# A transformer block on one core: four tiles for the split projections, the first maxima's rows and an exponential inside the projections, score products in attention's first two steps, and the first biases in the last unit

## The chip, the core and the metric

The kernel runs on one core of a Trainium2 chip. The metric is the device time of one launch in microseconds (us). TensorE is called PE here and its weight loads PEld; VectorE is DVE, ScalarE is ACT, GpSimd is POOL, and SP is the engine that issues most of the DMA transfers.

## What is computed

The reference is one block of a diffusion transformer with a conditioned layer norm, causal attention and an MLP, all in fp32. Here there are B = 2 rows of T = 2048 tokens with D = 512 channels, 16 heads of 32, and 2048 hidden channels.

```python
mod = silu(condition) @ Wada + bada
sh_a, sc_a, gt_a, sh_m, sc_m, gt_m = split(mod, 6, axis=1)
xm = layernorm(x, g1, be1) * (1.0 + sc_a[:, None, :]) + sh_a[:, None, :]
q, k, v = heads(xm @ Wqkv)
scores = where(causal, q @ k.T * hd ** -0.5, -inf)
attn = softmax(scores) @ v
x = x + gt_a[:, None, :] * (attn @ Wproj + bproj)
xm = layernorm(x, g2, be2) * (1.0 + sc_m[:, None, :]) + sh_m[:, None, :]
h = gelu(xm @ W1 + b1)
x = x + gt_m[:, None, :] * (h @ W2 + b2)
```

## The kernel before

**Stages.** For each of the two rows: the projections to q, k and v, then attention, then the out-projection; the MLP follows for both rows together. The out-projection of row 0 is `project_phase`, whose hook `between` prepares the projections of row 1.

**Projections** (`Qkv`). They run in four groups g of 512 tokens. `group` has twelve parts n: n = 0 to 7 are q and k for four sets of four heads in turn (`ps_qk`), n = 8 to 11 are the values (`ps_v`) of four token tiles. Each q or k is split in two: ACT writes the high part into `hl` (L808[...]), DVE the rest (L809), and SP stores both to DRAM (L814), from where q and k come back as `qst` and `kst` with the parts laid over the partitions. `hl` has two tiles. `load_x` fetches the tokens of the group after into four tiles `x` (L759), and `stats` (L212) takes their mean and variance on DVE. Row 1's projections also carry a preparation of the MLP's weights on POOL.

**Units and scores.** Attention works in 16 units per row, four heads by 512 queries: unit u is a head set c and a query block i, with the blocks in order 0, 1, 2, 3 for the first set and 0, 2, 1, 3 for the others. A unit has two kinds of products. The *score products* (`Row.score`, tiles `s`) are done ahead of time only to find each query's largest score: DVE reduces them with L452, or with L447 where the causal mask is added. They have two PSUM banks of their own, `ps_s`, and can borrow one of the others. When the last of a unit is reduced, `split` (L466 to L468) writes the maxima in two parts to `mhl`. `rows(u)` then transposes them on PE (`ps_m`), and DVE spreads them into `fold` (L512). Score products of the first three units are interleaved with the products of the projections' groups 1 to 3 (the hook `among`, and `count`, which says how many are due).

**Steps.** A unit with query block i has 4i + 3 *steps*, 144 per row in all. A step first puts the negative maxima into four banks with four *bias products* (st<-fold,sel), adds the products of keys and queries (st<-kst,qst, keys on the partitions), and lets ACT write the four exponentials `e` (L577). On the diagonal, POOL zeroes what the mask hides (L583, affine_select). The products with the values (`o`) follow LAG = 2 steps later, and those with ones (`sm`), which sum the exponentials, come after them; pairs or more of exponentials are first added into `ee` (L605), on POOL, in the last unit on DVE. `due` spreads the score products of later units, at most AHEAD = 3 units ahead, over the steps, by a table of costs written in the kernel. The limit is one unit shorter in a unit's first two steps:

```python
n = row.count(
    due(u, starts[u] + n_step) - QB // 2, u + AHEAD - (n_step < 2)
)
```

**The last unit and the out-projection.** In the last unit of a row, `prepare` runs once per step and loads and scales what the out-projection needs: the weight, the gate, the bias `bgate`, the first query block's output `at_s[0]` (times its inverse sums, L427), and the first four token tiles `xt_s`. These four lie in the old `kst` tile, and so appear as kst in the profile. The out-projection takes 16 token tiles n, four to each query block (k counts the blocks). For each one POOL adds the bias to the tokens (L972), PE multiplies (`ps_o`), DVE adds the two (L979), and one part of the next block's output is scaled (L985).

**Order.** Each engine runs its instructions in one order. That of the matmuls, and of what is wrapped in `act`, is the order written; a scheduler orders the rest, DMA issues on SP among them. Code lines at the spot of the change are shown below.

Of the kernel before, what the change touches and what calls it, by code (L numbers as in the profile page):

```python
# [8 lines left out]
F32 = mybir.dt.float32  # L9
F32R = mybir.dt.float32r  # L10
BF16 = mybir.dt.bfloat16
AF = mybir.ActivationFunctionType
ALU = mybir.AluOpType
# [4 lines left out]
P = 128  # L18
# [3 lines left out]
QB = 512  # L22
MT = 512
# [4 lines left out]
def dit_block_kernel(  # L28
# [36 lines left out]
    nc = tc.nc  # L65
# [5 lines left out]
    HC = P // HD  # L71
# [4 lines left out]
    LAG = 2  # L76
# [54 lines left out]
        nc.vector.tensor_copy(pick, pickc.unsqueeze(3).to_broadcast([P, 2, B, P]))  # L131


    first_sqrt = const.tile([P, 1], F32, tag="first", name="first")
    nc.scalar.activation(first_sqrt, eps, AF.Sqrt)


    cols = const.tile([P, 64], F32, tag="cols", name="cols")
# [63 lines left out]
    def act(ins):  # L202

        return tc.keep_in_program_order(ins)
# [78 lines left out]
    class Row:  # L283
# [125 lines left out]
        def prepare(self, n):  # L409

            if n == 3:
                self.prefetch()
            elif n == 5:
                ps = rows_of(ps_sp, 0, self.b, "s")
                self.rb_s = [self.old_queries() for _ in range(2)]
                self.gate = self.rb_s[1][:, 0, :]
                act(nc.vector.tensor_copy(self.gate, ps))
                act(nc.vector.tensor_tensor(bgate, bgate, self.gate, ALU.mult))
                nc.sync.dma_start(self.rb_s[0], wide_d[self.b][last_order[0]])
            if 6 <= n < 6 + C:  # L420
                w = self.wproj[:, n - 6, :]
                act(nc.vector.tensor_tensor(w, w, self.gate, ALU.mult))
            if n == 10:
                nc.sync.dma_start(self.rb_s[1], wide_d[self.b][last_order[1]])
            if 11 <= n < 11 + C:
                d, r = self.at_s[0][:, n - 11, :], self.rb_s[0][:, n - 11, :]
                act(nc.vector.tensor_tensor(d, d, r, ALU.mult))  # L427

# [98 lines left out]
    def attention_phase(row):  # L527
        b, vv, kst, qst = row.b, row.vv, row.kst, row.qst
        with pool(f"att{b}") as ap, pool(
# [136 lines left out]
            for u, (c, i) in enumerate(units):  # L666
                if NQ <= u + AHEAD < len(units):
                    row.load_queries(u + AHEAD)
                if u % NQ == 0 and c + 1 < C:
                    row.load_keys(c + 1, 0, NG)  # L670
                steps = len(steps_of[u])
                for n_step, tiles in enumerate(steps_of[u]):
                    last = n_step == steps - 1
                    if n_step == 0:
                        summed = set()
                        o = ps_op.tile([P, QB], F32, tag="o", name="o")
                        sm = ps_op.tile([P, QB], F32, tag="sm", name="sm")
                    ready = row.at

                    n = row.count(  # L680
                        due(u, starts[u] + n_step) - QB // 2, u + AHEAD - (n_step < 2)
                    )
                    es, rest = scores_t(u, n_step, n)
                    rest = len(row.todo) - rest
                    make_rows = False
                    if u + 1 < len(units) and row.rows_made == u + 1:
                        if last:
                            row.score(row.count(cum[-1], u + 1))
                        make_rows = last or (ready > u + 1 and n_step >= 1)
                    row.inverses(u, n_step)  # L690
                    if u == len(units) - 1:
                        row.prepare(n_step)
                    flush(now)
                    if make_rows:
                        row.rows(u + 1)
                    row.score(max(0, len(row.todo) - rest))

                    def tile_by_tile(dst, lhs, es, tiles, first, last):
                        at = 0
                        for n, (j, q) in enumerate(tiles):  # L700
                            products(
                                dst, lambda h: lhs(j, h), es, q, at,
                                first and n == 0, last and n == len(tiles) - 1,
                            )
                            at += QB - q

                    def values(es=es, tiles=tiles, c=c, o=o, first=n_step == 0, last=last):
                        tile_by_tile(
                            o,
                            lambda j, h: vv[:, j, (c * HC + h) * HD : (c * HC + h + 1) * HD],  # L710
                            es, tiles, first, last,
                        )

                    def row_sums(es, last, tiles=((0, 0),), sm=sm, summed=summed):
                        first = not summed
                        summed.add(len(summed))
                        tile_by_tile(sm, lambda j, h: ones[:, :HD], es, tiles, first, last)

                    pending.append((now + LAG, values))
                    sums_of, wait = None, 0  # L720
                    if n_step < i * TQ:
                        k = n_step % TQ
                        if k == 0:
                            even = es
                        elif k == 1:
                            chain = begin_chain(u, even, es)
                        else:
                            add_to(u, chain, es)
                        if k == TQ - 1 and n_step + 1 < i * TQ:
                            sums_of, wait = (chain, False), 2  # L730
                    elif i and n_step == i * TQ:
                        add_to(u, chain, es)
                        sums_of, wait = (chain, False), 2
                    else:

                        sums_of, wait = (es, last, tiles), i > 0 and not last
                    if sums_of:
                        pending.append(
                            (now + LAG + wait, lambda f=row_sums, s=sums_of: f(*s))
                        )  # L740
                    if last:
                        pending.append((now + LAG, lambda u=u, o=o, sm=sm: finish(u, o, sm)))
                    pending.sort(key=lambda p: p[0])
                    now += 1
            flush(now + LAG)

    class Qkv:
# [41 lines left out]
        def group(self, g, hp, between, among):  # L789
# [6 lines left out]
            for f in range(C):  # L796
                for which in range(2):
                    ps = psum.tile([P, MT], F32, tag="mm", name="ps_qk")
                    w0 = which * D + f * P
                    for k in range(C):  # L800
                        mm(
                            ps, w[:, k, w0 : w0 + P], xmT[:, k, :],
                            start=(k == 0), stop=(k == C - 1),
                        )
                        among(n, k)
                    hl = hp.tile([P, 2, MT], F32R, tag="hl", name="hl", bufs=2)
                    scale = HD**-0.5 if which == 0 else 1.0
                    nc.scalar.activation(hl[:, 0, :], ps, AF.Copy, scale=scale)  # L808
                    nc.vector.scalar_tensor_tensor(  # L809
                        hl[:, 1, :], ps, scale, hl[:, 0, :].bitcast(F32),  # L810
                        ALU.mult, ALU.subtract,
                    )
                    dst = (qd if which == 0 else kd)[b][f]
                    nc.sync.dma_start(  # L814
                        dst[:, :, tok].rearrange("l p t -> p l t"), hl.bitcast(F32)
                    )
                    between(n)
                    n += 1
                if f == 0:
                    row.load_keys(0, g)  # L820
                    row.load_queries(g)
# [12 lines left out]
        def run(self, hp, also):  # L834

            row = self.row
            for g in range(NG):

                def between(n):
                    if g + 1 < NG:  # L840
                        if n == 0 and g + 1 not in self.xts:
                            self.load_x(g + 1)
                        if n in (5, 8):
                            self.norm(g + 1, n // 8)()
                    also(g, n)

                def among(n, k):
# [13 lines left out]
                            )  # L861

                self.group(g, hp, between, among)
            row.rows(0)

    w1_v = W1.rearrange("(c p) f -> p c f", p=P)
    w2_v = W2.rearrange("(c p) f -> p c f", p=P)
# [62 lines left out]
    def project_phase(row, psum, between):  # L930
# [5 lines left out]
        with pool(f"proj{b}") as pp:  # L936
# [14 lines left out]
            for k, i in enumerate(last_order):  # L951
# [6 lines left out]
                for t in range(TQ):  # L958
# [10 lines left out]

                    tokens(n + 6)  # L970
                    nt, xt = rows_x[n], xts[n]
                    act(nc.gpsimd.tensor_tensor(xt, xt, bgate, ALU.add))  # L972
                    ps = psum.tile([P, D], F32, tag="mm", name="ps_o")
                    for c in range(C):
                        mm(
# [139 lines left out]
    attention_phase(row)  # L1115


    first, row = row, Row(1)
    with pool("qkv1") as qp, pool("ps_qkv1", bufs=6, space=PSUM) as ps_mm:
        qkv = Qkv(row, qp, ps_mm)  # L1120
        qkv.xts[0] = first.next_s

        def between(n):
            if n == 6:
# [8 lines left out]
            if n >= NT - MTT:  # L1133
                qkv.stats(1, n - (NT - MTT), True)

        project_phase(first, ps_mm, between)

        def also(g, n):
            if n % 4 == 1:
# [361 lines left out]
```

## Time and profile before

| | |
|---|---|
| runs | 2432.94, 2437.04, 2436.72 us, median 2436.72 |
| profiled execution | 2439.56 us, of which the span is 2437.9 |
| PE busy | 2394.4 us (98%), 10797 instructions |
| DVE, POOL, ACT busy | 1349.5 (55%), 1091.5 (45%), 893.7 (37%) |
| row 0: projections, attention, out-projection | 18.7 to 219.0, to 764.5, to 823.7 us |
| row 1: projections, attention, out-projection | 823.7 to 1021, to 1567, to 1626.5 us |
| MLP | 1626.5 to 2437 us |
| four exponentials / one POOL add / one select | 2.07 / 1.27 / 0.3 to 0.5 us |

In a timeline, a row gives the start and the length in us, the engine, the line, the operation with what it writes and reads, how many instructions are taken together, and in brackets how long the engine had been idle before and what released it. In a table of windows, a row gives for each engine the busy time and the number of instructions in that window, then PE's granted clock (1.00 is full speed), the mean busy share of the DMA engines, and GB/s. PE's matmul records are stretched while it waits for a bank or an operand, so a busy PE can still be one that waits.

### The profile page before, as it was taken

To read this page: it belongs to the slowest core of one execution; us is meant where nothing else is said; L and a number is where in the kernel's file an instruction comes from. 1 tells how busy PE (TensorE), PEld (TensorE's weight loads), DVE (VectorE), ACT (ScalarE), POOL (GpSimd) and SP (SyncE) were. 2 spreads that over 40 slices of the span, in tenths; PEclk is the share of its full clock that TensorE was granted. 3 is DMA by queue.
4 is the path that set the end of the run, shared out by engine and by line. 5 is a ranking of instruction groups with operands and counts; after the bars stand their busy time and mean duration, and the time that the engine had idled before them with its cause. 6 is when DMAs were issued, how large, how long until landed. Compare 5 with 4: busy or idle time off the path is not lost.

```text
span 2437.9 us, 31025 instructions
## 1 busy us (share of the span) xinstructions
PE 2394.4 (98%) x10797; PEld 1172.4 (48%) x10797; DVE 1349.5 (55%) x2836; ACT 893.7 (37%) x1668; POOL 1091.5 (45%) x1255
## 2 busy tenths in 40 slices
PE   8999999999999999999999999999999999999998
PEld 3445555555544444555555554444444444444443
DVE  3465766767657535567666665673354263343424
ACT  2212555555554021255555555423213212312310
POOL 1061997978773460089787879312002101100200
PEclk9999999999999999999999999999999999999999
DMA  7667115051325694530515122462234234222323
GB/s 227 218 224 194 41 39 114 23 113 45 104 95 207 211 303 158 149 67 23 123 35 113 45 78 105 145 204 76 87 99 132 88 96 141 82 91 94 115 85 99
DMA packets 132853, 285.72 MB, mean 117 GB/s; under 512 B 13472, under 2 KB 42700, under 8 KB 127832
## 3 DMA queue, kind: packets, MB, share of 16 engines
q1 hardware_dynamic: 126224, 257.46, 35.6%
q0 software_dynamic: 6384, 26.25, 3.0%
q8 instruction: 85, 1.39, 0.2%
q14 instruction: 72, 0.59, 0.1%
q10 hardware_dynamic: 88, 0.02, 0.0%
HBM read 209.76 MB, written 81.79 MB: 120 GB/s over the span
## 4 chain that ended last, share of the span: by engine, by line
PE 94%; DVE 2%; DMA 2%; POOL 1%; issue 1%; ACT 0%; DVEq 0%; SPq 0%; ACTq 0%; POOLq 0%
PE st L200 20%; PE ps_y L200 16%; PE ps_h L200 16%; PE o L200 11%; PE s L200 10%; PE ps_qk L200 9%; PE ps_o L200 4%; PE sm L200 4%; PE ps_v L200 4%; DMA k<-hl 1%; PE ps_xt L208 1%; POOL ee L605 1%; PE ps_o L208 0%; DVE junk L447 0%; DMA x<-in_x_dram 0%
## 5 line engine op out<-in xcount | busy, mean ns | idle before, releaser
L577 ACT ACTIVATE e<-st 128x512 f32<-128x512 f32 (+1 forms) x1152 | 573.8, 579 | 432.5 <-PE st L200 364.4
L605 POOL TENSOR_TENSOR ee<-ee,e 128x512 f32<-128x512 f32 x424 | 528.8, 1285 | 4.8 <-ACT e L577 4.5
L452 DVE TENSOR_REDUCE mx<-s 128x1 f32<-128x512 f32 x606 | 408.9, 688 | 206.3 <-PE s L200 205.3
L200 PE MATMUL s<-kst,qst 128*128 128x512 f32 (+3 forms) x1032 | 464.9, 452 | 9.0 <-DVE mx L447 4.2
L200 PE MATMUL st<-qst,kst 128*128 128x512 f32 (+3 forms) x1280 | 412.5, 390 | 0.0
L1272 POOL TENSOR_TENSOR c<-c 128x512 f32<-128x512 f32 x32 | 40.8, 1274 | 623.7 <-DVE c L1234 487.6
L200 PE MATMUL o<-e,vv 128*32 128x512 f32 (+3 forms) x2560 | 296.9, 540 | 2.0 <-POOL e L583 2.0
L447 DVE CUSTOM_DVE_ANT_0 junk<-s,causal 128x512 bf16<-128x512 f32 (+3 forms) x426 | 209.2, 491 | 147.1 <-PE s L200 139.1
L200 PE MATMUL ps_h<-sx,w 128*128 128x512 f32 x640 | 286.7, 592 | 0.0
L200 PE MATMUL ps_y<-sh,w 128*128 128x512 f32 x640 | 278.3, 595 | 0.0
L200 PEld LDWEIGHTS st<-qst,kst 128*128 128x128 f32 x1280 | 230.0, 190 | 94.9 <-issue 62.9
L200 PEld LDWEIGHTS s<-kst,qst 128*128 128x128 f32 x1032 | 194.9, 189 | 158.3 <-DVE mx L452 49.5
L605 POOL TENSOR_TENSOR ee<-e 128x512 f32<-128x512 f32 x168 | 210.3, 1284 | 105.6 <-ACT e L577 105.3
L200 PE MATMUL ps_qk<-xmT,wqkv 128*128 128x512 f32 x512 | 242.3, 601 | 2.2 <-DVE xmT L257 2.2
L583 POOL TENSOR_SCALAR_AFFINE_SELECT e<-e 128x128 f32<-128x128 f32 (+1 forms) x384 | 119.7, 347 | 255.8 <-ACT e L577 253.0
L1234 DVE TENSOR_TENSOR h<-c,ps_h 128x512 f32<-128x512 f32 x128 | 88.0, 688 | 232.4 <-PE ps_h L200 232.2
L200 PEld LDWEIGHTS ps_h<-sx,w 128*128 128x128 f32 x640 | 121.1, 190 | 150.2 <-issue 149.5
L200 PEld LDWEIGHTS ps_y<-sh,w 128*128 128x128 f32 x640 | 121.3, 191 | 148.9 <-issue 147.5
L1258 ACT ACTIVATE h<-h,cols 128x512 f32<-128x512 f32 x128 | 92.4, 722 | 182.0 <-DVE h L1234 182.0
L200 PE MATMUL st<-fold,sel 32*128 32x512 f32 (+1 forms) x1152 | 150.7, 483 | 2.1 <-DVE mhl L468 1.0
L200 PEld LDWEIGHTS ps_qk<-xmT,wqkv 128*128 128x128 f32 x512 | 95.0, 192 | 99.0 <-issue 92.6
L200 PEld LDWEIGHTS st<-fold,sel 32*128 32x128 f32 x1152 | 60.1, 182 | 148.1 <-ACT e L577 91.2
(128 smaller groups left out, 2325.8 us busy)
## 6 DMA issues: line engine op xcount, KB each, us to landing
qst<-q SPq DMA_DIRECT2D x128, 256.0 KB
w<-w1d SPq DMA_DIRECT2D x34, 896.0 KB
w<-w2d SPq DMA_DIRECT2D x28, 1024.0 KB
kst<-k SPq DMA_DIRECT2D x24, 1024.0 KB
q<-hl SPq DMA_DIRECT2D x32, 512.0 KB
k<-hl SPq DMA_DIRECT2D x32, 512.0 KB
kst<-k SPq DMA_DIRECT2D x32, 256.0 KB
w<-in_L_cond_W_dram POOLq DMA_DIRECT2D x64, 128.0 KB, 4.7
```

The costliest lines, as they stand in the source:

```text
L200: return tc.keep_in_program_order(nc.tensor.matmul(*args, **kw))
L208: return tc.keep_in_program_order(nc.tensor.transpose(dst, src, ident[:n, :n]))
L447: nc.vector.tensor_tensor_reduce(junk[:, :w], s[:, :w], causal[:, QB - w :], 1.0, MASKED, ALU.add, ALU.max, m,)
L452: nc.vector.tensor_reduce(m, s[:, :w], axis=AX.X, op=ALU.max)
L577: act(nc.scalar.activation(e[:, :w], sts[h][:, :w], AF.Exp))
L583: nc.gpsimd.affine_select(d, d, pattern=[[0, len(tiles)], [1, P]], compare_op=ALU.is_ge, fill=0.0, base=0, channel_multiplier=-1,)
L605: act(engine.tensor_tensor(dst, x, y, ALU.add))
L1234: nc.vector.tensor_tensor(dst, x, y, op)
L1258: nc.scalar.activation(d, d, AF.Gelu, bias=col(r_b1 + chunk, 1))
L1272: nc.gpsimd.tensor_tensor(c1_, c1_, c2_, ALU.subtract)
```

## The change

There are four edits, and a renaming (`first_sqrt` to `first`, and the row `first` to `past`). The tiles `hl` are four instead of two. The rows of the first unit's maxima are made in the last group of the projections, after its first value product, instead of behind the group, and ACT there takes one exponential of a column that nobody reads, so that its function table is loaded at that point. In the first two steps of a row's attention at least four score products may be placed, and unit 3, the third ahead, is open to them. POOL's four additions of the bias to the first block's tokens are issued in the last four steps of the last unit, in `prepare`, instead of in the out-projection.

```diff
--- before.py
+++ after.py
@@ -131,8 +131,8 @@
         nc.vector.tensor_copy(pick, pickc.unsqueeze(3).to_broadcast([P, 2, B, P]))
 
 
-    first_sqrt = const.tile([P, 1], F32, tag="first", name="first")
-    nc.scalar.activation(first_sqrt, eps, AF.Sqrt)
+    first = const.tile([P, 1], F32, tag="first", name="first")
+    nc.scalar.activation(first, eps, AF.Sqrt)
 
 
     cols = const.tile([P, 64], F32, tag="cols", name="cols")
@@ -423,6 +423,9 @@
             if n == 10:
                 nc.sync.dma_start(self.rb_s[1], wide_d[self.b][last_order[1]])
             if 11 <= n < 11 + C:
+
+                t = self.xt_s[n - 11]
+                act(nc.gpsimd.tensor_tensor(t, t, bgate, ALU.add))
                 d, r = self.at_s[0][:, n - 11, :], self.rb_s[0][:, n - 11, :]
                 act(nc.vector.tensor_tensor(d, d, r, ALU.mult))
 
@@ -678,8 +681,12 @@
                     ready = row.at
 
                     n = row.count(
-                        due(u, starts[u] + n_step) - QB // 2, u + AHEAD - (n_step < 2)
+                        due(u, starts[u] + n_step) - QB // 2,
+                        u + AHEAD - (n_step < 2 and u > 0),
                     )
+                    if u == 0 and n_step < LAG:
+
+                        n = max(n, HC)
                     es, rest = scores_t(u, n_step, n)
                     rest = len(row.todo) - rest
                     make_rows = False
@@ -803,7 +810,7 @@
                             start=(k == 0), stop=(k == C - 1),
                         )
                         among(n, k)
-                    hl = hp.tile([P, 2, MT], F32R, tag="hl", name="hl", bufs=2)
+                    hl = hp.tile([P, 2, MT], F32R, tag="hl", name="hl", bufs=4)
                     scale = HD**-0.5 if which == 0 else 1.0
                     nc.scalar.activation(hl[:, 0, :], ps, AF.Copy, scale=scale)
                     nc.vector.scalar_tensor_tensor(
@@ -842,6 +849,10 @@
                             self.load_x(g + 1)
                         if n in (5, 8):
                             self.norm(g + 1, n // 8)()
+                    elif n == 8:
+
+                        row.rows(0)
+                        act(nc.scalar.activation(first, eps, AF.Exp))
                     also(g, n)
 
                 def among(n, k):
@@ -861,7 +872,6 @@
                             )
 
                 self.group(g, hp, between, among)
-            row.rows(0)
 
     w1_v = W1.rearrange("(c p) f -> p c f", p=P)
     w2_v = W2.rearrange("(c p) f -> p c f", p=P)
@@ -969,7 +979,8 @@
 
                     tokens(n + 6)
                     nt, xt = rows_x[n], xts[n]
-                    act(nc.gpsimd.tensor_tensor(xt, xt, bgate, ALU.add))
+                    if k > 0:
+                        act(nc.gpsimd.tensor_tensor(xt, xt, bgate, ALU.add))
                     ps = psum.tile([P, D], F32, tag="mm", name="ps_o")
                     for c in range(C):
                         mm(
@@ -1115,10 +1126,10 @@
     attention_phase(row)
 
 
-    first, row = row, Row(1)
+    past, row = row, Row(1)
     with pool("qkv1") as qp, pool("ps_qkv1", bufs=6, space=PSUM) as ps_mm:
         qkv = Qkv(row, qp, ps_mm)
-        qkv.xts[0] = first.next_s
+        qkv.xts[0] = past.next_s
 
         def between(n):
             if n == 6:
@@ -1133,7 +1144,7 @@
             if n >= NT - MTT:
                 qkv.stats(1, n - (NT - MTT), True)
 
-        project_phase(first, ps_mm, between)
+        project_phase(past, ps_mm, between)
 
         def also(g, n):
             if n % 4 == 1:
```

## The prediction

> **What bounds the kernel now.** I read the chain of waits first, then busy time and granted clock in windows cut at the stages, then the timelines of the places where PE stops or slows, and the chain behind each.
>
> ```profile
> PE 94%; DVE 2%; DMA 2%; POOL 1%; issue 1%; ACT 0%; DVEq 0%; SPq 0%; ACTq 0%; POOLq 0%
> ...
> 18.70:219.00 200.30, 195.87 (x566) 95.66 (x566) 98.68 (x238) 36.11 (x66) 41.24 (x60) 0.99 0.66 210
> 219.00:240.00 21.00, 19.99 (x104) 10.83 (x103) 7.63 (x18) 9.62 (x18) 3.95 (x12) 0.76 0.89 188
> 240.00:764.50 524.50, 521.34 (x3568) 269.38 (x3566) 356.29 (x849) 295.40 (x591) 425.90 (x479) 1.00 0.28 74
> ...
> 223.88:227.29 3.41, 3.41 (x10) 2.47 (x10) 0.00 (x0) 1.81 (x5) 1.11 (x4) 0.50 1.02 207
> 227.29:230.71 3.42, 3.42 (x13) 2.53 (x13) 1.51 (x3) 1.90 (x5) 1.54 (x5) 0.50 0.96 196
> 230.71:234.12 3.41, 3.41 (x19) 0.85 (x18) 1.33 (x3) 0.66 (x2) 0.83 (x3) 0.50 1.05 226
> ...
> 882.59:886.00 3.41, 3.41 (x6) 1.33 (x4) 0.85 (x3) 0.00 (x0) 1.83 (x4) 0.51 0.98 363
> ```
>
> After the times come the engines PE, PEld, DVE, ACT, POOL, then clock, DMA share and GB/s. PE owns the chain, so only PE's stops and slow stretches can be won. The attention body runs at clock 1.00, but its first 21 us hold 0.76: three windows at half clock (row 1 the same, 1025.94 to 1036.17, 0.50). One more lies in row 1's projections.
>
> ```profile
> 161.11 0.60 ACT L808 ACTIVATE hl<-ps_qk 128x512 fp32r<-128x512 f32 x1 [2.74 <-DMA k<-hl]
> 163.27 0.50 PE L200 MATMUL s<-kst,qst 128*128 128x512 f32 x1 [2.32 <-DVE mx L452]
> 221.57 0.51 PE L200 MATMUL st<-fold,sel 32*128 32x512 f32 x4 [1.01 <-DVE mhl L468]
> 879.85 0.69 DVE L212 BATCH_NORM_STATS2 stat<-x 128x6 f32<-128x512 f32 x1 [3.26 <-DMA x<-in_x_dram]
> 881.61 0.44 PE L200 MATMUL s<-kst,qst 128*128 128x384 f32 x1 [3.39 <-DVE mx L447]
> ```
>
> PE's stops name a DVE reduction. What held DVE is ahead of it in its own queue: the low half of hl (L809), which waits for ACT's high half (L808), which waits until an earlier hl has been stored.
>
> **1. hl in four tiles.** Nothing is added to any engine; ACT's and DVE's turns for a tile come two tiles later. Row 0: chain DMA k<-hl 155.14 + 5.89, ACT, DVE, PE at 163.27; the 2.32 goes whole: a tile takes eight products of 0.43 (ps_qk 4.29 per ten in the chain), 3.4 us, so four span 13.7. Row 1: hl's stores took 15.09 (from 846.00) and 8.71 us (863.29), which held SP back, so that the x load left only at 873.87 and DVE's L212 waited for it until 879.85. The 3.39 goes, and with it half of the half-clock window 882.59:886.00, 1.7 us. The edit reorders SP: in row 1 three x loads stand behind the next group's first q store instead of around the last k stores, and on DVE their L212 come behind two reductions of that group. At 875.5 (first q done) plus the landing of 5.89 they are there by 882. DVE then frees the third score bank, which PE wants for its fifth product; by row 0's spacing (71.84, 72.81, 74.64, 77.40, 83.12) that is 11.3 us after 874.85, at 886. The 15.09 can still outlast 13.7; ACT's 1.4 is then covered by the projections' six banks. So nothing new should stop PE; I allow 1.0 for a partial wait over both rows. If the cover of 4 us fails, each us of lateness beyond it is one of PE. Sum -7.4 + 1.0 = -6.4; bounds -7.5 and, with a new wait as long as the old one in row 1 (3.39 + 1.7) and none gone in row 0, about 0.
>
> **2. First maxima's rows and an Exp inside the projections.** Before, the transpose ps_m comes after the last value product (220.29), the fold (L512, DVE 0.83) follows, and PE stands 1.01 (row 1: 0.92 at 1022.95). Afterwards both lie among the last group's products, where a transpose of 0.27 goes between score products and 0.83 on a DVE half idle (98.68 of 200.30) costs nothing. PE can then start the bias products at once, but the third waits for a bank that the last value copy (ACT 220.49 to 221.07) frees, so 0.55 of each gap is won: -1.1 over both rows. The table load (1.28 at 221.09) ends at 222.37, before the first product is there: the first exp starts 0.17 behind it. Moving it gains nothing by this row; ACT is 18% busy where it goes.
>
> **3. Score products in the first two steps.** The instruction order before and after gives, per row, score products in steps 0 and 1: 0 and 0 before, 5 and 5 after; in steps 36 and 37 (the next head group's first two): 5 and 4 before, 0 and 0 after; in between the counts move by one, from step 38 on they are equal. Both places are PE's. At 36 and 37, nine products of 0.225 (a 512-wide one there) are 2.0 us; steps start at 359.74, 363.56, 369.20, and ACT's four exps (2.07) fit in what is left, so PE can run 2.0 earlier. Against it: POOL works from 324.59 to 363.98 without a pause over 0.6 and its twelve selects (3.49 from 360.49) release the next value products; I take 1.8 per row. At steps 0 and 1 the added 2.2 us fall into PE's waits for exps (ACT 2.07 per four, PE's own work 1.7), so they cost little: step 0 to step 3 lasts 13.0 us in the trace (221.57 to 234.58), of which 7.4 would be work at full clock.
>
> The clock decides the rest. The window 220.47 to 223.88 ahead of those at half clock holds the 1.01 gap and waits for banks; by counting instructions at their unhindered times PE truly worked some 47% of it. Elsewhere a gap of 2.32 (163.27) and one of 1.73 (782.83) were followed by no drop; that last one left about 51% idle at worst. So what tips the clock here is near half a window. With edits 2 and 3 I count 65 to 70% of work in these windows. The page "TensorE: Matmul & The Clock Gate" of the Trainium skill, section "Part 1: The HAM clock gate", speaks against it: half clock follows a whole idle window of about 3.4 us, and its end table asks for no gaps over about 3 us. By that rule neither the 1.01 gap nor this filling matters, the drop has some other cause and stays, and edit 3 is worth about -2.0 per row with edit 2. By the trace (3.39 agrees with the rule, 1.01 contradicts it) the drop goes: I lay the steps out at full clock with the ten products and reach step 3 2.7 us earlier than 234.58 (the 0.55 of edit 2 in it). I take the trace: -2.7 - 1.8 = -4.5 per row, -9.0 over both for edits 2 and 3. Bounds -3.4 (clock still halves, part of steps 36 and 37 given back) and -11.
>
> **4. First biases earlier.** Four POOL adds per row move from the out-projection (L972, 4.97 from 761.87) into the last unit's last four steps. Where they were, they hid: DVE's first use (L979, 768.33) waits for PE, and POOL stands until 770.71 afterwards. So leaving costs and wins nothing. Where they go, each (1.24) stands in POOL's queue between the selects of one step and the next: the first in 34.83 us of idle before 755.40, harmless; the second behind 757.5, delaying the eight selects of 758.08 by about 0.7; the third delays the last four by up to 1.5. The value products that wait for them start 760.02 and 763.49, behind other products. For DVE's two-input adds in the same stretch (L605 0.69, L427 0.69), the nearest rows are L985 next to L972: 0.66 alone, 1.66 and 2.49 beside POOL's. The page "SBUF — State Buffer", section "SBUF: two separate sides", names it an exclusive lock between POOL and two-input DVE operations, for the whole instruction: by it each bias can cost DVE 1.24, five us of DVE time per row; by the rows 1.0 to 1.8 for one that meets. L427's last is due only for the products at 764.52 and was done by 760.27, so 4 us cover it. I put +0.3 per row, bounds 0 and +1.5; a gain is excluded since the adds were hidden.
>
> The renaming costs nothing. **Sum:** -6.4 - 9.0 + 0.6 = -14.8 against the profiled execution's 2439.56 (span 2437.9 and 1.66 around it): 2424.8. That execution lies 2.84 above the median of the runs, 2436.72, so on their scale 2421.9; I say 2422.5. Runs spread over 4 us, so a difference of 0.2% (4.9 us) is about what a measurement can tell from no change.
>
> **The rivals.**
> - Main case, 0.56: both halves hold, 2418 to 2427, middle 2422.5.
> - The clock still halves at the start, or POOL gives steps 36 and 37 back, 0.24: edits 2 and 3 bring -4 instead of -9, and 2436.7 - 6.4 - 4 + 0.6 = 2427. For it: the page's rule, and POOL's 39 us without a pause. Against: occupancy over the level of 782.83, where no drop came.
> - DVE waits for the later x loads, 0.13: edit 1 brings 0 to -3 and the clock part is partly lost too: 2436.7 - 1.5 - 4 + 0.6 = 2431.8. For it: DMA share 0.97 to 1.06 around 880, stores of up to 15 us. Against: 4 us of cover.
> - Slower, 0.07: one mechanism, the x loads that now follow a group's first q store, three places in all (two in row 0, one in row 1). If they land after the 15.09 that a store took there, instead of 5.89, they come at 890.6, DVE frees the bank at 891.6 instead of by 886, PE stands 5.6 and half of a window at half clock (1.7) follows: 7.3 a place. Two places give 2421.5 (the sum without its allowance) + 14.6 = 2436, no change; all three 2443. So it decides from a landing near 14.5 us at all three. Against: the loads around 157 to 164 landed with 5.89 at 301 GB/s.
> - That the change does not do what it says is small: the order of instructions shows the ten products, the four tiles and the earlier rows.
>
> **How the numbers follow.** Faster by over 0.2% is below 2431.8: the main case, the second, and half of the third less tails, 0.80. Within 0.2%: the rest of the third and the near side of the fourth, 0.13. Slower: 0.07. The range takes in the main case with edit 3's deep bound, the second, and the middle of the third: 2417 to 2432.5.
>
> **What would show it.** Right: no PE gap over 1 us at about 163 and 880; ACT no longer waiting for DMA q or k<-hl; first bias products directly behind the last value products, granted clock near 1.0 there; steps 0 to 3 in about 10 us; steps 36 and 37 shorter by 2. Wrong: clock 0.50 at the start of attention again, DVE L212 waiting for DMA x by over 3 us with PE behind it, POOL's selects named as releaser at the value products of steps 35 to 37, or out-projection products waiting for L427.

## The result, and the profile after

The changed kernel takes 2424.3 us (median of 4 runs, 2422.69 to 2425.71), the kernel before beside it 2436.88 (2432.94 to 2438.42): a ratio of 0.9951, with a 95% interval of 0.9933 to 0.9968. The prediction was 2422.5, range 2417 to 2432.5. The profiled executions went from 2439.56 to 2424.88, -14.7, where the sum said -14.8. That these two agree is in part luck. By the stretches of the table below, the projections won 9.3 us (1.07 and 8.26) where the `hl` term said 6.4, attention up to its last step 9.2 where 9.0 was said, and the ends of the last units lost 3.8 where 0.6 was said: two errors of opposite sign. And the profiled execution before lies 2.7 us above its kernel's median; from median to median the change won 12.6 us, where the prediction had 14.2 (2436.72 to 2422.5).

Windows of the changed kernel: 21 us at each start of attention (first two rows; row 0's is the window shown before), and a stretch of row 0's projections:

```profile
219.00:240.00 21.00, 19.94 (x139) 11.48 (x139) 14.50 (x34) 11.39 (x23) 7.10 (x15) 1.00 0.96 199
1010.00:1031.00 21.00, 20.18 (x141) 11.40 (x140) 15.23 (x34) 11.65 (x24) 7.38 (x15) 1.00 0.91 192
...
133.11:136.52 3.41, 3.41 (x8) 1.65 (x7) 1.12 (x4) 0.00 (x0) 2.16 (x4) 0.60 1.06 327
```

PE's clock at the start of attention is 1.00 in both rows (0.76 before in row 0), with 139 PE instructions in row 0's 21 us instead of 104. A stretch at reduced clock now lies at 133 us, where the profile before had none.

The timeline of the changed kernel at the places where PE had stopped:

```profile
220.06 0.50 PE L200 MATMUL st<-fold,sel 32*128 32x512 f32 x2 [0.24 <-ACT vv L837]
877.93 1.29 DVE L212 BATCH_NORM_STATS2 stat<-x 128x6 f32<-128x512 f32 x2 [2.87 <-DMA x<-in_x_dram]
880.66 0.62 PE L200 MATMUL s<-kst,qst 128*128 128x128 f32 x1
```

The gap of 1.01 at the start is 0.24, ended by the bank of the last value copy, as the prediction said. DVE does wait for late x loads, 2.87 us here and 7.11 us ahead of 869.19, longer than the 3.26 before the change. But PE's fifth score product of that group, 880.66, comes without a wait, and the third, at 874.54, after one of 0.34.

Progress tells where the time went. Each figure is how far the profiled execution is ahead (minus) of the one before at that point, in us; e1 is the run with the bias additions put back, e2 the kernel before with four `hl` tiles alone:

| point | before at | changed | e1 | e2 |
|---|---|---|---|---|
| row 0, last value product ends | 220.46 | -1.07 | -3.32 | -3.09 |
| row 0, step 3 | 234.58 | -3.79 | -6.05 | -6.39 |
| row 0, step 36 | 359.74 | -3.52 | -5.81 | -6.19 |
| row 0, step 38 | 369.20 | -4.58 | -6.87 | -6.21 |
| row 0, step 143 (the last) | 759.04 | -4.72 | -7.04 | -6.68 |
| row 0, first out-projection product | 764.52 | -2.82 | -7.03 | -6.68 |
| row 1, last value product ends | 1021.93 | -11.08 | -15.67 | -14.71 |
| row 1, step 3 | 1036.33 | -14.82 | -19.41 | -14.73 |
| row 1, step 38 | 1171.04 | -15.78 | -20.34 | -14.85 |
| row 1, step 143 | 1561.42 | -16.66 | -21.14 | -15.76 |
| row 1, first out-projection product | 1566.91 | -14.78 | -21.14 | -15.76 |

In the changed kernel 1.9 us are lost between step 143 and the first out-projection product, in both rows alike. The same stretch of the trace, with the additions on POOL (L428) among the selects (L586):

```profile
750.69 2.92 POOL L586 TENSOR_SCALAR_AFFINE_SELECT e<-e 128x128 f32<-128x128 f32 x4 [16.39 <-ACT e L580]
752.01 3.84 DVE L608 TENSOR_TENSOR ee<-ee,e 128x512 f32<-128x512 f32 x4 [0.19 <-POOL e L586]
753.59 1.71 POOL L428 TENSOR_TENSOR kst<-kst,bgate 128x512 f32<-128x512 f32 x1
755.25 2.83 POOL L586 TENSOR_SCALAR_AFFINE_SELECT e<-e 128x256 f32<-128x256 f32 x4
755.31 3.34 PE L200 MATMUL o<-e,vv 128*32 128x512 f32 x19
```

and before:

```profile
758.08 3.82 POOL L583 TENSOR_SCALAR_AFFINE_SELECT e<-e 128x256 f32<-128x256 f32 x8 [0.56 <-ACT e L577]
760.02 1.98 PE L200 MATMUL o<-e,vv 128*32 128x512 f32 x24
```

At the same progress (4.72 us earlier) the first of step 13's selects would start at 753.36; it starts at 755.25. PE's value products, which wait for the selects, are stretched from 1.98 for 24 to 3.34 for 19.

### The profile page after: what moved, and what is told of

Same layout as the page of the kernel before. It is cut to its first block, busy times and chain, and to the rows that moved or that the text cites. A ratio compares the mean times of both kernels' runs of the same rounds, so it can differ in the third digit from the quotient of the medians.

```text
span 2423.1 us, 31009 instructions
## 1 busy us (share of the span) xinstructions
PE 2388.1 (99%) x10797; PEld 1169.3 (48%) x10797; DVE 1358.6 (56%) x2836; ACT 895.1 (37%) x1670; POOL 1096.5 (45%) x1255
## 4 chain that ended last, share of the span: by engine, by line
PE 95%; DVE 3%; POOL 1%; DMA 1%; issue 1%; ACT 0%; SPq 0%; DVEq 0%; POOLq 0%; ACTq 0%
PE st L200 19%; PE ps_y L200 16%; PE ps_h L200 16%; PE o L200 11%; PE s L200 10%; PE ps_qk L200 8%; PE ps_v L200 4%; PE ps_o L200 4%; PE sm L200 4%; PE ps_xt L208 1%; POOL ee L608 1%; DMA x<-in_x_dram 1%; PE ps_o L208 0%; DVE junk L450 0%; DVE mx L455 0%
## 5 line engine op out<-in xcount | busy, mean ns | idle before, releaser
L586 POOL TENSOR_SCALAR_AFFINE_SELECT e<-e 128x128 f32<-128x128 f32 (+1 forms) x384 | 122.2, 356 | 200.5 <-ACT e L580 197.8
```

The lines of the kernel that those rows point to most:

```text
L586: nc.gpsimd.affine_select(d, d, pattern=[[0, len(tiles)], [1, P]], compare_op=ALU.is_ge, fill=0.0, base=0, channel_multiplier=-1,)
```

## The experiments

**e1: the bias additions put back.**

```diff
-                t = self.xt_s[n - 11]
-                act(nc.gpsimd.tensor_tensor(t, t, bgate, ALU.add))
...
-                    if k > 0:
-                        act(nc.gpsimd.tensor_tensor(xt, xt, bgate, ALU.add))
+                    act(nc.gpsimd.tensor_tensor(xt, xt, bgate, ALU.add))
```

> The changed kernel, with the four bias additions back in the out-projection. Theory (they stand in POOL's queue between the last selects and slow DVE's additions by meeting them): in the profiles the lead over the kernel before shrinks from 4.72 to 2.82 us (row 0) and from 16.66 to 14.78 (row 1) between the last step's bias products and the first out-projection product, so about 3.8 us come back: 2424.3 - 3.8 = 2420.5, and the stretch from step 143 to the first ps_o lasts 5.5 us as before the change, not 7.4. Rival (the end of the last unit is late because DVE or the scores are later for another reason of the change): 2424, and the stretch stays at 7.4.

2418.91 us, ratio 0.9923 (0.9907 to 0.9940): the fastest of the versions that ran more than once. The last stretch takes 5.49 us in both rows, as the theory said, against 7.38 and 7.37 in the changed kernel: the edit costs 3.8 us. Its median is 5.4 below the changed kernel's. In the profiles the rest lies in row 0's projections (2.25 us, table), where every engine has the same instructions in the same order, and which the last run takes up.

**e5, e9, e10: the additions elsewhere, and one by one.** e5 moves all four to steps 7 to 10, where POOL has nothing else to do:

```diff
-            if 11 <= n < 11 + C:
+            if 7 <= n < 7 + C:
+                t = self.xt_s[n - 7]
+                act(nc.gpsimd.tensor_tensor(t, t, bgate, ALU.add))
```

> The changed kernel with the four bias additions in steps 7 to 10 of the last unit instead of 11 to 14, where POOL has no selects to do. Theory (the 1.9 us per row came from POOL's queue: bias additions between the selects): nothing stands before the selects, the stretch from step 143 to the first ps_o is 5.5 us or little more, 2419 to 2420.5 as with the additions in the out-projection. Rival (it came from DVE: in the changed kernel the first addition, at 732.64, stretched DVE's four additions from 2.49 to 3.58 us, and DVE is then busy to the end of the unit; four such meetings put it 4.4 us back, as much as its last scaling has in hand): the stretch is 7 us or more, 2423 to 2426.

2427.33 us (ratio 0.9961, 0.9945 to 0.9976), and the stretch takes 9.32 and 9.31 us: twice the loss, so the rival was right, and its price even too low. e5's timeline:

```profile
731.70 5.77 DVE L609 TENSOR_TENSOR ee<-e 128x512 f32<-128x512 f32 x4
731.86 6.74 POOL L427 TENSOR_TENSOR kst<-kst,bgate 128x512 f32<-128x512 f32 x4 [16.78 <-DVE bgate L418]
749.91 10.32 POOL L587 TENSOR_SCALAR_AFFINE_SELECT e<-e 128x128 f32<-128x128 f32 x12 [11.30 <-ACT e L581]
```

The gate that the bias needs (L418) ends only as DVE starts its additions, so all four POOL additions come at once and meet them. DVE's four take 5.77 instead of 2.49. DVE then has no pause until the unit's end; its additions, now over 3 us late, run beside POOL's twelve selects, and these take 10.32 us, where before, as in e1, the three groups of them added up to 5.74 (0.29 + 1.63 + 3.82).

e9 keeps only the first addition early (`if n == 11`), e10 only the other three (`if n > 11`):

> The changed kernel with only the first bias addition in the last unit (step 11), the other three in the out-projection. It stands in POOL's idle time, so it can only act through DVE, whose four additions beside it took 3.58 instead of 2.49 us. Theory A (DVE, once late, meets POOL's selects at the end of the unit, and both get longer): most of the 1.9 us between step 143 and the first ps_o is there, 6.5 to 7.4 us instead of 5.5. Theory B (POOL's queue: the second and third addition stand before selects): 5.5 us.

> The changed kernel with the first bias addition in the out-projection and the other three in the last unit (steps 12 to 14). Theory A (DVE late from the first one): the stretch from step 143 to the first ps_o is near 5.5 us. Theory B (POOL's queue): 7 us or more, with the eight selects of step 13 about 1.3 to 1.9 us behind their exponentials.

The stretch takes 6.15 us in both rows of e9 and 6.57 in both of e10 (one execution each, 2417.88 and 2421.2 us). Against 5.49 without any, the first alone costs 0.66, the others 1.08, together 1.74 of the 1.89 measured: each theory holds for a part. e9's timeline, then e10's:

```profile
730.22 3.58 DVE L609 TENSOR_TENSOR ee<-e 128x512 f32<-128x512 f32 x4
730.38 1.66 POOL L429 TENSOR_TENSOR kst<-kst,bgate 128x512 f32<-128x512 f32 x1 [16.78 <-DVE bgate L418]
748.43 7.16 POOL L587 TENSOR_SCALAR_AFFINE_SELECT e<-e 128x128 f32<-128x128 f32 x12 [16.39 <-ACT e L581]
```

```profile
730.36 2.49 DVE L609 TENSOR_TENSOR ee<-e 128x512 f32<-128x512 f32 x4
750.66 1.70 POOL L429 TENSOR_TENSOR kst<-kst,bgate 128x512 f32<-128x512 f32 x1
752.32 2.83 POOL L587 TENSOR_SCALAR_AFFINE_SELECT e<-e 128x256 f32<-128x256 f32 x4
```

In e9 the addition stands in idle time of POOL's, 16 us ahead of any select, and still delays the last products: 1.09 us late on DVE (3.58 against 2.49) come out as a longer block of selects 18 us later. In e10 DVE is in time, and what delays the selects is the addition in front of them.

**e2, e6, e8: the hl tiles.** e2 is the kernel before with four; e6 is e1 with two, which leaves the rows, the exponential and the scores alone; e8 is e1 with three.

```diff
-                    hl = hp.tile([P, 2, MT], F32R, tag="hl", name="hl", bufs=2)
+                    hl = hp.tile([P, 2, MT], F32R, tag="hl", name="hl", bufs=4)
```

> The kernel before, with four hl tiles and nothing else. Theory (the store waits of hl held DVE, DVE held PE): the gaps of 2.32 and 3.39 us and the half clock after the second go, 2.3 + 5.1 = 7.4 us, and some shorter waits: 2436.9 - 7 to 9 = 2428 to 2430; the start of attention keeps its three windows at half clock. Rival (most of the gain is made at the start of attention, and the gaps come back elsewhere as waits for x): 2434 or more, with DVE's L212 waiting for DMA x over 3 us.

> As the run with the additions put back (2418.9), but with two hl tiles: the early rows, the exponential and the score products alone on the kernel before. Theory (the two halves add up, hl worth 3.1 us in row 0 and 8.0 in row 1, the rest some 9): 2418.9 + 11 = 2430, granted clock near 1.0 at both starts of attention, gaps of 2.3 and 3.4 us back in the projections. Rival (the two overlap, since a kernel with four tiles alone already ran at 2422.5): 2424 to 2426.

> As the run with the additions put back (2418.9), with three hl tiles. Theory (a tile is wanted again after three times 3.4 us or somewhat more, and most stores land in 6 to 9 us): row 0 as with four; in row 1, where a store took 15 us, ACT still waits for one or two stores, so 1 to 3 us of the 8 there are lost: 2420 to 2422. Rival (two tiles' wait is only moved, row 1 loses most): 2425 or more. Rival (three are enough): 2418.9.

| kernel | median us | ratio (95%) | row 0, end of group 0 to end of group 3 | row 1, first out-projection product to end of group 3 |
|---|---|---|---|---|
| before, 2 tiles | | | 155.78 | 257.41 |
| e6, 2 tiles | 2429.68 | 0.9969 (0.9960 to 0.9978) | 155.22 | 254.16 |
| e8, 3 tiles | 2424.80 | 0.9949 (0.9932 to 0.9967) | 154.09 | 250.19 |
| e1, 4 tiles | 2418.91 | 0.9923 (0.9907 to 0.9940) | 152.38 | 248.77 |
| e2, 4 tiles | 2422.51 | 0.9944 (0.9927 to 0.9961) | 152.18 | 249.38 |

e2 alone is already where the changed kernel is, 6 us below what its own theory expected, and far below its rival's 2434. Part of that is the half clock that did not come in row 0's attention, against the theory (next part). The tiles are worth 3.6 us in row 0 and 8.0 in row 1 against the profile before (2.3 and 5.1 predicted for the two gaps). PE's waits from the start of row 0's projections to the end of row 1's show what was missed; before, then e2:

```profile
PE s L200 <- DVE mx L447: 3.8, 2, 3.4
PE s L200 <- DVE mx L452: 3.0, 3, 2.3
PE ps_v L200 <- ACT xmT L262: 2.1, 5, 0.7
PE ps_xt L208 <- ACT vv L830: 1.0, 4, 0.2
```

```profile
PE s L200 <- DVE mx L447: 0.8, 1, 0.8
PE s L200 <- DVE mx L452: 0.4, 1, 0.4
```

The columns are the waiting instruction, what ended the wait, then us in total, times, and the longest. (Of the first two rows of before some 0.9 us, and e2's 0.4, lie between the two projections.) The last two rows of before, 3.1 us in nine small pieces, are gone in e2. One place of four, before and in e2:

```profile
53.12 0.66 PE L208 MATMUL ps_xt<-ident,xn 128*128 128x128 f32 x4 [0.24 <-ACT vv L830]
```

```profile
53.85 1.04 PE L208 MATMUL ps_xt<-ident,xn 128*128 128x128 f32 x8
```

These are the transposes of the next group's tokens (`ps_xt`), behind a group's first value product. ACT does not stand before an `hl` here: it had been idle for 9.14 us ahead of that value copy, at 52.48. But with two tiles, four of the group's eight q and k are still unread in their PSUM banks; with four tiles, two or fewer. The projections have six such banks (`bufs=6`): with the value product and the first half of the transposes they are full, and the second half waits until the copy frees one (0.24); the modulation (L262) and the next value products are late behind it (0.34). In each of the four places and at the fifth wait (0.73, ahead of 959.06) four were unread before. That the banks are what is short follows from these counts; no run changed their number.

Against e6 the tiles are worth 2.8 and 5.4 us: how long the stores take differs, and the long gaps were 1.53 and 1.64 there instead of 2.32 and 3.39. With three tiles 1.4 of the 5.4 in row 1 is not won. In row 0 it is 1.7, but 1.6 of it lies in the one group in which e8 held a stretch at half clock, from 134 us (group 2, 56.7 us against e1's 55.1), so that is not the price of the fourth tile. e6 came out at the 2430 that its theory had, with the clock at 1.00 at both starts of attention, though with shorter gaps than it expected. e8's median is near the 2425 of its first rival, 5.9 above e1's, and its profile does not show that the missing tile costs that much. Together, e6's gain (8 us) and the tiles' (15 alone) would give 23, and e1 has 18.8: the halves overlap by some 4 us, and the next part says where most of it lies.

**e3, e4, e11: the start of attention.** e3 is the changed kernel without the ten score products, e4 without the early rows and exponential, e11 is e2's kernel once more.

```diff
-                        u + AHEAD - (n_step < 2 and u > 0),
+                        u + AHEAD - (n_step < 2),
...
-                    if u == 0 and n_step < LAG:
-                        n = max(n, HC)
```

```diff
-                    elif n == 8:
-                        row.rows(0)
-                        act(nc.scalar.activation(first, eps, AF.Exp))
...
+            row.rows(0)
```

> The changed kernel without the score products in the first two steps. Theory (PE's clock falls at the start of attention because PE works too small a share of those windows, and the ten products fill them): half clock comes back for about three windows in both rows, and steps 0 to 3 last 13 us instead of 11.4; with the 1.0 us per row at steps 36 and 37 that also goes back, 2424.3 + 2 x (2 to 3) = 2428 to 2430. Rival (the 1.0 us gap alone tipped the clock, and the earlier rows of maxima remove it): clock 1.00, steps 0 to 3 about 1.5 us shorter than with the ten products, which then come back later: 2424 to 2425.

> The changed kernel with the first unit's rows of maxima behind the projections again and without the early exponential. Theory (the ten products fill the windows; the gap in itself is only its length): the gap of 1.0 is back, clock stays 1.00 or nearly, 2424.3 + 2 x 0.6 to 1.0 = 2425.5 to 2426.3. Rival (the gap tips the clock): half clock for one to three windows in each row, 2424.3 + 2 x (2 to 4) = 2428 to 2432.

> The same kernel as the run with four hl tiles alone, a second execution. There the granted clock stayed at 1.00 at the start of row 0's attention (step 0 to step 3 in 9.7 us) and fell to 0.50 for 11 us in row 1 (12.9 us), with the same instructions and the same gap of 1.01 us before both. Theory (where the thin start falls against PE's clock windows differs from one execution to the next): the pair comes out otherwise in this one, in about half of executions for each row, 9.7 or 13 us. Rival (it is a property of the program at that place): row 0 full and row 1 half again.

e3: 2428.54 us (0.9958, 0.9942 to 0.9975), as its theory said. e4: 2423.71 (0.9946, 0.9931 to 0.9960), with the clock that its theory expected, and faster than it expected. e11: 2423.6, one execution. Steps 0 to 3, with the clock in a window over them:

| | gap ahead | score products in steps 0, 1 | row 0 us, clock | row 1 us, clock |
|---|---|---|---|---|
| before | 1.0 | none | 13.01, 0.61 | 13.38, 0.62 |
| e2 | 1.0 | none | 9.70, 1.00 | 13.26, 0.61 |
| e11 | 1.0 | none | 9.70, 1.00 | 13.03, 0.61 |
| e3 | closed | none | 13.33, 0.74 | 11.99, 0.72 |
| e4 | 1.0 | ten | 10.71, 1.00 | 10.73, 1.00 |
| changed | closed | ten | 11.47, 1.00 | 10.73, 1.00 |

e4's gap in row 1 and its clock there, from the timeline and the windows of e4:

```profile
1009.97 0.50 PE L200 MATMUL st<-fold,sel 32*128 32x512 f32 x4 [1.01 <-DVE mhl L471]
```

```profile
1009.97:1020.70 10.73, 9.92 (x60) 5.92 (x60) 8.04 (x17) 6.40 (x13) 3.95 (x12) 1.00 1.00 215
```

and e2's two starts, the same instructions behind the same gap:

```profile
218.49:228.19 9.70, 9.48 (x49) 5.05 (x50) 2.71 (x4) 6.29 (x13) 3.94 (x12) 1.00 1.00 211
1008.34:1021.60 13.26, 13.26 (x48) 6.98 (x48) 2.85 (x4) 6.49 (x13) 3.94 (x12) 0.61 0.99 213
```

So the gap is not what tips the clock: with it and the ten products the clock holds, without it and without them it falls. With them it held in all twenty starts profiled (ten executions of nine kernels); without them it fell in six of eight. Where the thin start keeps its clock (e2, row 0) it is the faster one, 9.70 against 10.7 to 11.5. So the ten products cost 1.0 to 1.8 us at the start, win some 1 us at steps 36 and 37 (8.40 from step 36 to 38 against 9.46), and what they bring beyond that is a clock that no longer falls. This is most of the overlap: e2's row 0 had that part for nothing (3.3 us between the last value product and step 3).

e11 did not come out otherwise, as its theory wanted; row 0 held and row 1 fell again, as its rival said. But the traces speak for the theory's reason. In each trace the half-clock stretches begin whole multiples of 3.413 us apart (in the profile before, those at 223.88, 882.65 and 1026.01 are 193 and 42 of them apart, to 0.01 us), and where this grid lies against the program differs between executions. In the two thin starts that held, a window of the grid began 0.79 us (e2) and 0.72 us (e11) behind step 0; in the four that fell behind such a gap it began 0.35 to 1.11 us ahead of step 0. (e3, without the gap, fell with both: 0.48 ahead and 1.00 behind.) So e2 and e11 came out alike because their windows happened to lie alike. The twenty filled starts did not hold by such luck: their windows began anywhere from 1.69 us ahead of step 0 to 1.59 behind it. The closest pair is row 1 of e2, 0.59 us ahead, and of e4, 0.60 us ahead, both behind a gap of 1.01; that window and the next, e2's two rows, then e4's:

```profile
1007.76:1011.17 3.41, 2.83 (x11) 1.44 (x11) 0.51 (x2) 3.23 (x6) 0.80 (x3) 1.00 0.84 202
1011.17:1014.58 3.41, 3.41 (x11) 2.60 (x10) 0.00 (x0) 1.80 (x5) 1.17 (x4) 0.50 0.98 199
...
1009.37:1012.78 3.41, 2.64 (x13) 1.83 (x13) 2.14 (x5) 3.23 (x6) 0.78 (x3) 1.00 0.83 199
1012.78:1016.19 3.41, 3.26 (x18) 2.32 (x17) 2.91 (x9) 2.33 (x5) 1.60 (x5) 1.00 1.02 207
```

e2's runs spread from 2420.76 to 2430.14 with the mean clock falling from 0.997 to 0.993, those of before from 2430.11 (0.997) to 2445.16 (0.991), while e1's stay within 4.4 us. That fits, but only profiled executions show their windows, and no run could set where they lie.

**e7: no early exponential**, on e1.

> As the run with the additions put back (2418.9), without the early exponential, so that ACT loads its table before the first real one. Theory (the load lay behind the gap before; with the gap gone its 1.28 us end about 0.4 us after the first products are there): PE's next bias products wait that long, 0.4 us per row, 2419 to 2420. Rival by the page 'ScalarE: Activation LUTs' (2.7 us with its drain): 2424. Rival (it is still hidden): no difference, 2418.9.

2422.35 us (0.9939, 0.9922 to 0.9957); in its profile it loses 0.26 us in row 0 and 0.98 in row 1 from the last value product to step 3. In e7's row 1:

```profile
1008.30 1.28 ACT L578 ACT_TABLE_LOAD   x1
...
1010.25 0.50 PE L200 MATMUL st<-kst,qst 128*128 128x512 f32 x1 [0.58 <-ACT e L578]
```

The first exponential comes 0.29 us later behind step 0 than in e1 in row 0, and 1.03 in row 1 (where no bias product has to wait for the last value copy), and PE waits for it. So the early load does win something, though only because the fold came early too. Its median stands 3.4 us above e1's, which is more than this explains; the two profiled executions are 1.0 apart, and e7's runs spread over 4.5 us.

**e12: the changed kernel again.**

> The changed kernel itself, a second execution. In the first one row 0's projections ended only 1.07 us earlier than before the change, and 3.3 us earlier in the run with the biases put back, which has the same instructions up to there; the first one held two stretches at half clock (17 to 25 us and 133 to 137 us) where the other held one. Theory (these come and go between executions): one or both are shorter or gone, and the projections end 2 to 3.3 us earlier than before; the start of attention is at full clock again, step 143 to the first ps_o lasts 7.4 us again. Rival (something in the last unit or in the layout of the changed kernel does it): 1.1 us and the same two stretches.

2423.83 us, one execution: row 0's projections end 1.68 us early instead of 1.07, less than the theory wanted; the stretch at 133 us is there again, the one at 17 to 25 us shorter. Step 143 to the first out-projection product takes 7.4 us again. The stretch at 133 us was in five of the fourteen profiles (changed, e12, e3, e5, e8), in none of e1, e2, e4, e6, e7, e9, e10, e11 and before. Ahead of it PE has a gap of 0.95 us and many small products in every kernel. Where the windows lie separates the two kinds here too: in the five that fell, one began 1.09 to 1.38 us ahead of the end of that gap; in the nine others the nearest began 1.59 us ahead (e4), or between 1.01 us ahead and 0.14 behind. The changed kernel fell there twice, and e1 and e9, with the same instructions in the same order up to there, did not; so it comes and goes with the execution. This is read from the traces and not tested.

## Why the prediction held, and where it didn't

- *hl in four tiles, -6.4.* The mechanism was right, both gaps and the half clock behind the second are gone, and the later x loads cost PE little: DVE waits up to 7.11 us, over the 3 that the prediction had named as a sign of being wrong, but PE stands behind it for 0.34 alone, less than the 1.0 allowed. The size was off: e2 has 11.6 (3.6 and 8.0) against 6.4, and the changed kernel 9.3, with its stretch at 133 us. The term looked only at the two long gaps, and left out that q and k which wait for a tile hold PSUM banks that the next group's transposes want (3.1 us in nine waits of PE).
- *Early rows and exponential, -0.55 per row.* The gap closed down to 0.24. e4, without both, needs 0.4 us more in row 0 and 1.2 in row 1 from the last value product to step 3 (11.83 and 11.85 against 11.40 and 10.66); e7, with the rows alone, needs 11.65 and 11.64, so the rows alone win 0.2. In the medians none of it shows: e4 has 2423.71, the changed kernel 2424.30. "Moving it gains nothing" was wrong for the exponential: by the row before the load was hidden, but by the gap that this very change takes away.
- *Score products, -4.5 per row with the rows.* From the last value product to step 143 the changed kernel gained 3.65 and 5.58 us, 9.2 against 9.0. Of row 1's, 0.9 lies behind step 38, where e2, without these edits, gains as much; so some 8.3 is the fairer figure. Within it, the start gave 2.7 as predicted and 3.7; steps 36 to 38 gave 1.05 instead of 1.8. There the work is gone, but PE's bias products, which took 0.62 and 0.50, now take 1.07 per four (timeline of the changed kernel):

```profile
356.22 1.07 PE L200 MATMUL st<-fold,sel 32*128 32x512 f32 x4
359.35 1.07 PE L200 MATMUL st<-fold,sel 32*128 32x512 f32 x4
```

  The fourth of each waits for its bank: at step 36 until 356.76 for DVE, which still reduces a score product there, at step 37 until 359.89 for ACT's exponential. That takes back half. The choice between rule and trace went the right way. The rule cited there, from the section "Part 1: The HAM clock gate" of the Trainium skill's page "TensorE: Matmul & The Clock Gate", has half clock come behind an idle window of about 3.4 us; here it came six times with no gap over 1.01 us, so the measurement decides. The prediction put the cure down to both edits together; e3 and e4 show that the filling does it, not the closing of the gap. And it took the two drops for fixed. In e2 and e11 row 0 kept its clock without the change, so what this term won there hung on where the windows of the profile before lay: that part is luck.
- *Biases, +0.3 per row, bounds 0 and +1.5.* This step failed: +1.9 per row. "The first in 34.83 us of idle, harmless" looked at POOL alone; it was not free because the gate that it waits for is what DVE's own stream waits for too, so it always meets DVE's additions. That 4 us of slack were found for L427 was beside the point: the late DVE additions met the selects, and PE waits for the selects. The lock that the Trainium skill's page "SBUF — State Buffer" describes (section "SBUF: two separate sides") was cited for its cost on DVE, and not followed back to POOL. e5 comes close to such taking of turns: four additions of each engine, 7.46 us one after the other, took 6.90 from the first start to the last end.

## What to carry to other kernels

An instruction moved into an engine's idle time is free only if it does not slow the work of another engine beside it (here POOL's additions and DVE's), or if what it delays has slack up to the next thing that the critical engine reads. A buffer that is freed late costs more than the wait that names it: what waits for it holds other buffers, so sum the critical engine's small waits too before pricing the long one. A gain from a clock that fell in one profiled execution is worth only as much as it falls in the others. And a hidden piece of work is hidden by something: when one change removes the cover, price the piece again.

## What the runs showed of the hardware

- PE's clock fell to 0.50 for 7 to 10 us behind a start in which PE mostly waits for banks, in six of eight starts, with no gap over 1.01 us and, while it was down, with records that call PE fully busy; filled with ten products more it held at 1.00 in twenty of twenty.
- The half-clock stretches of a trace lie on a grid of 3.413 us. The same instructions fell or held by where that grid lay: at the thin start behind a gap (fell in four, held in two) and at 133 us (fell in five, held in nine).
- A POOL addition beside DVE's two-input additions: four of each, 2.49 and 4.97 us alone, took 5.77 and 6.74 together. POOL's selects are slowed beside DVE's additions too, 10.32 instead of 5.74 for twelve, which no estimate had in it.
